# Two pixel chunks per projection to dt's input, B and C in the last layer of a four-layer kernel

## The chip, the cores and the metric

The kernel runs on one core of a Trainium2 chip. A core has a matrix engine (TensorE, PE in the profile), a vector engine (VectorE, DVE), a scalar engine (ScalarE, ACT), a general one (GpSimd, POOL) and a queue engine (SyncE, SP) that issues the DMA transfers here. The metric is device time of one execution in microseconds (us), lower is better; the number compared is the median over runs.

## The reference

Four layers follow each other on an input of 4 images with 192 channels and 56 x 56 pixels, all in fp32: an attention layer with a 7 x 7 convolution, a channel gate, a window-attention layer, and a selective scan in four directions. Only the last is touched:

```python
xn = _ln_cf(x, ln_w, ln_b)
xc, z = jnp.split(jnp.einsum('dc,bchw->bdhw', in_proj_w, xn), 2, axis=1)
xc = jax.nn.silu(depthwise_3x3(xc, conv_w) + conv_b)
x_hw = xc.reshape(Bsz, D, L)
x_wh = xc.transpose(0, 1, 3, 2).reshape(Bsz, D, L)
xs = jnp.stack([x_hw, x_wh, x_hw[..., ::-1], x_wh[..., ::-1]], axis=1)
x_dbl = jnp.einsum('kcd,bkdl->bkcl', x_proj_w, xs)
dts, Bv, Cv = jnp.split(x_dbl, [R, R + N], axis=2)
dt = jax.nn.softplus(jnp.einsum('kdr,bkrl->bkdl', dt_proj_w, dts) + dt_proj_b[None, :, :, None])
# for each pixel: h = exp(dt * A) * h + dt * B * u ; y = sum over N of h * C
ys = _selective_scan(xs, dt, A, Bv, Cv) + Ds[None, :, :, None] * xs
out = x + out_proj(layer_norm(sum over the four directions of ys) * silu(z))
```

(`depthwise_3x3`, `out_proj` and the sum over directions are written short here.) `x_dbl` is what the change is about: for each direction 12 + 4 + 4 = 20 rows, so for the two directions that run along rows (forth and back) 40 rows from the same pixels, and 40 more for the two that run along columns.

## The kernel before

All four layers are one program. Each layer's work is written as generators (threads) that yield what they need next: an engine, an estimated cost and the tiles to take. `Order` (line 270) keeps a clock of its own, at each turn picks among the first 130 threads the one that can begin earliest (a thread's place weighs 0.05 us each), and emits its instructions. The outcome is a fixed order of instructions on every engine; SP's queue gets its transfers in the order of emission. So any edit of a cost, a tile count or a condition may change the order of everything that comes after it.

In the last layer (`layer3`, line 1990) an image is cut into 7 chunks of 8 pixel rows, 448 pixels. Channels lie as two halves of 96 partitions, padded with zeros to 128.

- `begin(b, c)` (line 2103) loads one chunk of the previous layer's output, does the layer norm (L2079, L2081, L2089, L2094, L2097, L2098, L2100), the projection to x and z (L2134), the bias (L2145), the 3 x 3 convolution (L2167) and SiLU into the image's `u` (L2184), and SiLU of z (L2194), which is stored to `zmem` (L2199). The convolution's output lags by a pixel row, so the row pieces are 392, 5 x 448 and 504 pixels. Then `product` (line 2210) makes the 40 rows of `x_dbl` for that piece: two accumulating matmuls (L2218) into one PSUM bank, a copy to a `prod` tile (L2221; two such tiles, given at L2065) and a store to `prods` in DRAM (L2224). The flag `("rows", b, c)` is set.
- `begin_columns(b, c)` (line 2204) waits until all seven row pieces of the image are in, and calls `product` for eight pixel columns, read from `u` and written to the bank transposed. It sets `("columns", b, c)`.
- The scans are 28 steps per image: rows forth, columns forth, columns back, rows back, 7 chunks each. `load(t)` (line 2279) waits for the flags, for rows of chunk c also those of chunk c + 1, because of the lag; it loads dt's input (`dr`, L2289), and B and C broadcast over partitions (`bc`, L2295), from `prods`. `sizes` (line 2300) takes two steps at a time, and begins when both are loaded: matmul to dt (L2310) and softplus (L2322). `decay` (line 2337) spreads dt over the states by DMA (`da`, L2348) and takes the exponential (L2356). `scan(t, h)` (line 2359), for each half h of the channels, makes dt * u (`du`, L2371 or L2374), spreads it by matmul (L2381), multiplies by B (L2387), runs the scan on DVE (L2403), multiplies by C on POOL (L2410), sums over the states by three matmuls to three column tiles of 32 (L2426), and adds to `y` (L2431, L2436, L2440).
- `final(b, c)` (line 2227) normalises, gates by z and projects out (L2254, L2265).

The places given at lines 2452 to 2463 put `begin` of image b in the 56 half steps of image b - 1, with column products from place 48 on; for image 0 `begin` overlaps the end of the layer before.

Of the kernel before, what the change touches and what calls it, by code (L numbers as in the profile page):

```python
# [22 lines left out]
B, C, H, W = 4, 192, 56, 56  # L23
HW = H * W
HALF = 96
CH = 448
NCHUNK = HW // CH
# [214 lines left out]
def load_packs(nc, pool, packs, aps, names=None):  # L242
    tiles = {}
    for name, pack in packs.items():
        if names is not None and name not in names:
            continue
        t = pool.tile([pack.p, pack.n], F32, name=f"w_{name}", bufs=1)
        nc.sync.dma_start(t, aps[name])
        for n in pack.at:
            tiles[name + "." + n] = pack.view(t, n)  # L250
    return tiles
# [18 lines left out]
class Order:  # L270
# [29 lines left out]
    def take(self, kind="bank"):  # L300
        slot = min((s for s in self.kinds[kind] if s[0] is not None), key=lambda s: s[0])
        slot[0] = None
        return slot[1]

    def done(self, tile):

        (slot,) = (s for slots in self.kinds.values() for s in slots if s[1] is tile)
        slot[0] = self.end + self.LATENCY
# [57 lines left out]
def on_pe(n, *takes, ready=None):  # L366

    return "PE", 0.0019 * n, takes, None, ready
# [14 lines left out]
def on_act(*n, takes=(), table=None, ready=None):  # L383
    return "ACT", sum(0.2 + 0.0009 * i for i in n), takes, table, ready
# [6 lines left out]
def on_sp(*takes):  # L391
    return "SP", 0.5, takes, None, None
# [1597 lines left out]
def layer3(tc, order, pools, src, packs, aps, dst):  # L1990
# [7 lines left out]
    nc = tc.nc  # L1998
# [7 lines left out]
    w = load_packs(nc, const, packs, aps)  # L2006
# [10 lines left out]
    def keep(name, shape, n, rows=128, pool=const):  # L2017
        return [pool.tile([rows, *shape], F32, name=f"{name}{i}") for i in range(n)]

    rows = keep("row", [2, CH], 4)  # L2020
    sqs = keep("sq", [2, CH], 2)
    pads = keep("pad", [2, 11, W + 2], 2)
    us = keep("u", [2, HW], 1)
    drs = keep("dr", [SCH], 3)
# [16 lines left out]
    for m in range(4):  # L2041
        for k in range(2):
# [4 lines left out]
                start=(k == 0),  # L2047
                stop=(k == 1),
# [13 lines left out]
    yield on_dve(24, 2)  # L2062
    nc.vector.tensor_scalar_mul(a_neg, a_neg, -1.0)
    nc.vector.tensor_reduce(d_sum, w["c96.Ds"], AX.X, ALU.add)
    order.give(row=rows, sq3=sqs, dr=drs, gate=keep("gate", [2, CH], 2, HALF), prod=keep("prod", [512], 2, 40))  # L2065
    y = None
    prods = [[dram.tile([40, HW], F32, name=f"prod{b}_{o}") for o in range(2)] for b in range(B)]
    zmem = [dram.tile([C, HW], F32, name=f"zmem{b}") for b in range(B)]
    passed = set()

    def gone(*what):
        return what in passed
# [30 lines left out]
    def begin(b, c):  # L2103
# [9 lines left out]
        u = us[b % 2]  # L2113
# [4 lines left out]
        i = NCHUNK * b + c  # L2118
# [35 lines left out]
        n = y1 - y0  # L2154
        at = y0 - (8 * c - 1)
        px = slice(y0 * W, y1 * W)
        pc = None
        for t in range(9):
# [3 lines left out]
            for h in range(2):  # L2162
                for s in range(2):
                    for r in range(3):
                        o = 32 * (2 * h + s)
                        x = 28 * s + t % 3
# [4 lines left out]
                            start=(t == 0),  # L2171
                            stop=(t == 8),
                        )
        uv = u[:, :, px].rearrange("p h (y x) -> p h y x", x=W)
# [4 lines left out]
        for r in range(3):  # L2179
            yield on_act(*[28 * n] * 4, table=SILU)  # L2180
            for h in range(2):
                for s in range(2):
                    o = 32 * (2 * h + s)
# [14 lines left out]
        yield on_sp()  # L2198
        nc.sync.dma_start(pixels(zmem[b])[:, :, c * CH : (c + 1) * CH], zt)  # L2199
        done(zt)  # L2200
        yield from product(b, 0, px, u[:, :, px], 2)
        passed.add(("rows", b, c))

    def begin_columns(b, c):
        yield lambda: all(gone("rows", b, i) for i in range(NCHUNK))
        uv = us[b % 2].rearrange("p h (y x) -> p h y x", x=W)[:, :, :, 8 * c : 8 * c + 8]
        yield from product(b, 1, slice(c * CH, (c + 1) * CH), uv, 2)
        passed.add(("columns", b, c))

    def product(b, o, px, u, passes):  # L2210

        n = px.stop - px.start
        yield on_pe(passes * n, "bank")
        pp = take()

        out = pp[:40, :n].rearrange("p (x y) -> p y x", y=H) if o else pp[:40, :n]
        for k in range(2):
            nc.tensor.matmul(out, w["c128.xpT"][:, k, o], u[:, k], start=(k == 0), stop=(k == 1))  # L2218
        yield on_act(n, takes=("prod",))
        t = take("prod")  # L2220
        nc.scalar.copy(t[:, :n], pp[:40, :n])  # L2221
        done(pp)
        yield on_sp()
        nc.sync.dma_start(prods[b][o][:, px], t[:, :n])  # L2224
        done(t)

    def final(b, c):

        px = slice(c * CH, (c + 1) * CH)
        yield lambda: gone("summed", b, c) and (c == NCHUNK - 1 or gone("read", b, c + 1))  # L2230
        yield on_sp("row", "row", "gate")
        yn, xl, sz = take("row"), take("row"), take("gate")
        nc.sync.dma_start(sz, pixels(zmem[b])[:, :, px])
        yield from layer_norm(y[:, :, px], yn, read=("read", b, c))
        for h in range(2):
            yield on_act(CH)
            nc.scalar.activation(
                yn[:HALF, h],
                yn[:HALF, h],
                AF.Identity,  # L2240
                bias=w["c96.out_norm_b"][:, h : h + 1],
                scale=w["c96.out_norm_w"][:, h : h + 1],
            )
        yield on_pool(2 * CH, each=0.0021)
        nc.gpsimd.tensor_mul(yn[:HALF], yn[:HALF], sz)
        done(sz)
        yield on_sp()
        nc.sync.dma_start(xl[:HALF], pixels(src[b])[:, :, px])
        tiles = []
        for h in range(2):  # L2250
            yield on_pe(2 * CH, "bank", ready=order.end - 0.5)
            po = take()
            for k in range(2):
                nc.tensor.matmul(  # L2254
                    po[:HALF, :CH],
                    w["c128.outT"][:, k, HALF * h : HALF * h + HALF],
                    yn[:, k],
                    start=(k == 0),
                    stop=(k == 1),
                )  # L2260
            tiles.append(po)
        done(yn)
        for h in range(2):
            yield on_dve(CH)
            nc.vector.tensor_add(xl[:HALF, h], xl[:HALF, h], tiles[h][:HALF, :CH])  # L2265
            done(tiles[h])
        yield on_sp()
        nc.sync.dma_start(pixels(dst[b])[:, :, px], xl[:HALF])
        done(xl)
# [179 lines left out]
    def add(place, gen):  # L2449
        order.add(place + BASE3, gen, "3")  # L2450


    n = 8 * NSC
    for b in range(B):
        for c in range(NCHUNK):
            add(n * (b - 1) + 6 * c + 4, begin(b, c))
            add(n * (b - 1) + 48 + c, begin_columns(b, c))
            add(n * (b + 1) - 2 * c, final(b, c))
    for t in range(len(steps)):
        add(2 * t - 5, load(t))  # L2460
# [14 lines left out]
    y = late.tile([128, 2, HW], F32, name="y")  # L2475
# [13 lines left out]
def build(packs, extra):  # L2489
    nc = bacc.Bacc("TRN2", target_bir_lowering=False, num_devices=1)  # L2490

    def dram_in(name, shape):
        return nc.dram_tensor(name, shape, F32, kind="ExternalInput").ap()

    x = dram_in("x", [B, C, HW])
    aps = [{n: dram_in(n, [p.p, p.n]) for n, p in layer.items()} for layer in packs]
    aps[0].update({n: dram_in(n, list(a.shape)) for n, a in extra.items()})
    out = nc.dram_tensor("out", [B, C, HW], F32, kind="ExternalOutput").ap()
    with tile.TileContext(nc) as tc:
        with tc.tile_pool(name="between", bufs=1, space=DRAM) as dram:  # L2500
            x1 = [dram.tile([C, HW], F32, name=f"x1_{b}") for b in range(B)]
            x2 = [dram.tile([C, HW], F32, name=f"x2_{b}") for b in range(B)]
            pools = {k: ExitStack() for k in ("dram", "banks", "01", "01 sums", "2", "2 quads", "3")}
            order = layers01(tc, pools, [x[b] for b in range(B)], packs[0], aps[0], x1)
            order.add(84, layer2(tc, order, pools, x1, packs[1], aps[1], x2), "later")
            order.add(240, layer3(tc, order, pools, x2, packs[2], aps[2], [out[b] for b in range(B)]), "later")
            engines = {mybir.EngineType.PE, mybir.EngineType.Activation, mybir.EngineType.DVE, mybir.EngineType.Pool}
            with tc.manual_schedule(engines=engines):
                order.run()
            for k in ("3", "banks", "dram"):  # L2510
                pools[k].close()
    return nc
# [12 lines left out]
```

## Time and profile before

| | us |
|---|---|
| median of 3 runs | 5715.48 (5711.06 to 5721.34) |
| the profiled execution | 5731.28 |
| its span, first to last instruction | 5729.5 |
| PE busy over the span | 4866.4 (85%) |
| DVE busy over the span | 4140.6 (72%) |
| ACT busy over the span | 2655.4 (46%) |
| POOL busy over the span | 1699.9 (30%) |
| first and last matmul of L2218 begin at | 3881.4 and 5220.9 |
| first scan of the last layer (L2403) begins at | 3989.5 |

The span is the time from the first to the last instruction of one profiled execution; sums made from its rows are compared with its own time. "Busy" is the time in which an engine has at least one instruction under way. A row of the groups names a line, an engine, an operation, the tile written and the tiles read with their shapes, a count, the busy time and the mean time of one; after the bar stands the time for which the engine was idle just before, and who ended it. A chain of waits goes back from the last instruction to what released each.

### The profile page before, as it was taken

To read this page: it belongs to the slowest core of one execution; us is meant where nothing else is said; L and a number is where in the kernel's file an instruction comes from. 1 tells how busy PE (TensorE), PEld (TensorE's weight loads), DVE (VectorE), ACT (ScalarE), POOL (GpSimd) and SP (SyncE) were. 2 spreads that over 40 slices of the span, in tenths; PEclk is the share of its full clock that TensorE was granted. 3 is DMA by queue.
4 is the path that set the end of the run, shared out by engine and by line. 5 is a ranking of instruction groups with operands and counts; after the bars stand their busy time and mean duration, and the time that the engine had idled before them with its cause. 6 is when DMAs were issued, how large, how long until landed. Compare 5 with 4: busy or idle time off the path is not lost. (4 is left out here: it accounts for less than half of the span.)

```text
span 5729.5 us, 137267 instructions
## 1 busy us (share of the span) xinstructions
PE 4866.4 (85%) x58114; PEld 2407.0 (42%) x58114; DVE 4140.6 (72%) x6600; ACT 2655.4 (46%) x4271; POOL 1699.9 (30%) x1688
## 2 busy tenths in 40 slices
PE   4988998998899687898898888868888888888777
PEld 2444554454454444555555555534332232222112
DVE  5788447544744026888988888883678999998997
ACT  0122323212232215555555555546776776676544
POOL 0000000000000013433333433321345555555564
PEclk9999998999999798999999999989998999999998
DMA  6132224333332521000000000002456656566654
GB/s 185 53 80 60 66 60 105 64 88 91 76 69 56 99 77 37 14 22 21 17 22 18 19 20 21 16 26 60 122 135 157 160 145 172 155 149 167 165 149 109
DMA packets 356373, 475.97 MB, mean 83 GB/s; under 512 B 43600, under 2 KB 354256, under 8 KB 355248
## 3 DMA queue, kind: packets, MB, share of 16 engines
q1 hardware_dynamic: 355760, 467.20, 32.9%
q8 instruction: 458, 7.50, 0.5%
q14 instruction: 155, 1.27, 0.1%
HBM read 249.73 MB, written 63.17 MB: 55 GB/s over the span
## 5 line engine op out<-in xcount | busy, mean ns | idle before, releaser
L2410 POOL TENSOR_TENSOR da<-st,bc 128x448 f32<-128x448 f32 x672 | 857.0, 1281 | 751.5 <-DVE st L2403 600.1
L731 PE MATMUL bank<-X,wu 64*49 64x392 f32 x6720 | 610.5, 509 | 89.2 <-DVE X L710 85.9
L2403 DVE TENSOR_TENSOR_SCAN st<-da,st,bank 128x448 f32<-128x448 f32 x576 | 646.3, 1133 | 4.3 <-POOL da L2410 1.8
L838 POOL TENSOR_TENSOR attn<-attn,rs 112x1568 f32<-112x1568 f32 (+1 forms) x24 | 67.1, 2795 | 1726.5 <-DVE rs L836 989.9
L2356 ACT ACTIVATE da<-da,a_neg 128x448 f32<-128x448 f32 x672 | 410.1, 659 | 161.9 <-DMA da<-dt 150.2
L357 ACT ACT_TABLE_LOAD x373 | 478.6, 1283 | 6.6
L2387 DVE TENSOR_TENSOR bank<-bank,bc 128x448 f32<-128x448 f32 x672 | 382.9, 618 | 83.4 <-PE bank L2381 78.2
L731 PEld LDWEIGHTS bank<-X,wu 64*49 64x49 f32 x6720 | 247.6, 123 | 416.1 <-issue 366.4
L2426 PE MATMUL bank<-da,w_c 128*32 128x448 f32 x1344 | 348.8, 575 | 85.3 <-POOL da L2410 66.3
L2381 PE MATMUL bank<-du,w_c 32*128 32x448 f32 x1344 | 291.1, 643 | 105.2 <-DVE du L2371 59.2
L1569 DVE SCALAR_TENSOR_TENSOR bxn<-bapad,w_b,bxn 96x448 f32<-96x448 f32 (+2 forms) x448 | 318.7, 756 | 0.0
L1026 ACT ACTIVATE hm<-bank,w_a 128x448 f32<-128x448 f32 x168 | 106.3, 633 | 435.6 <-PE bank L1017 428.2
L1032 PE MATMUL bank<-hm,w_a 128*96 128x448 f32 x672 | 285.1, 555 | 16.7 <-ACT hm L1026 16.6
L1017 PE MATMUL bank<-xc,w_a 128*128 128x448 f32 x672 | 283.4, 551 | 0.6 <-DVE xc L998 0.6
L1430 POOL TENSOR_TENSOR bsq<-bsq 128x448 f32<-128x448 f32 (+7 forms) x120 | 144.5, 1206 | 446.9 <-ACT bsq L1427 401.8
L678 ACT ACTIVATE q<-bank,qk_bias,qk_scale 128x280 f32<-128x280 f32 (+2 forms) x216 | 116.9, 544 | 294.4 <-PE bank L664 251.2
L2134 PE MATMUL bank<-row,w_c 128*96 128x448 f32 x448 | 206.5, 599 | 29.7 <-DVE row L2100 27.9
L1488 PE MATMUL bank<-bxn,w_b 128*96 128x336 f32 (+2 forms) x576 | 214.3, 498 | 19.0 <-DVE bxn L1440 16.7
L754 ACT COPY sm<-bank 128x392 f32<-128x392 f32 x96 | 43.0, 489 | 380.6 <-PE bank L731 368.2
L2381 PEld LDWEIGHTS bank<-du,w_c 32*128 32x128 f32 x1344 | 92.1, 199 | 299.7 <-DVE du L2371 76.0
L998 DVE SCALAR_TENSOR_TENSOR xc<-bank,w_a,xc 96x224 f32<-96x224 f32 x112 | 44.9, 441 | 226.3 <-PE bank L988 124.5
L1763 PE MATMUL bank<-bzpad,b_diag 32*32 32x224 f32 (+2 forms) x8064 | 182.7, 371 | 24.1 <-ACT bzpad L1735 12.7
(333 smaller groups left out, 10015.4 us busy)
## 6 DMA issues: line engine op xcount, KB each, us to landing
da<-dt SPq DMA_DIRECT2D x672, 224.0 KB
vb<-vmem SPq DMA_DIRECT2D x576, 98.0 KB
bc<-prod SPq DMA_DIRECT2D x224, 224.0 KB
xq<-x SPq DMA_DIRECT2D x132, 210.0 KB
xc<-x SPq DMA_DIRECT2D x56, 336.0 KB
row<-x SPq DMA_DIRECT2D x56, 336.0 KB
xs<-x SPq DMA_DIRECT2D x28, 336.0 KB
vmem<-vt SPq DMA_DIRECT2D x56, 168.0 KB
```

The costliest lines, as they stand in the source:

```text
L357: self.nc.scalar.preload_act_table_set(table)
L731: nc.tensor.matmul(pm[a][outs[i], : WIN * W].rearrange("p (y x) -> p y x", x=W), wu[halves[a], k, dx], xt[halves[a], :, i, dx : dx + W], s ...
L1017: nc.tensor.matmul(ph[:, :CH], w["a128.c1T"][:, k, 128 * m : 128 * m + 128], xt[:, k], start=(k == 0), stop=(k == 1),)
L1032: nc.tensor.matmul(acc[h][:HALF, :CH], w["a128.c2T"][:, m, HALF * h : HALF * h + HALF], hm, start=(m == 0), stop=(m == 5),)
L1488: nc.tensor.matmul(rows2(pq[:HALF, :m]), w["b128." + wn][:, k, HALF * h : HALF * h + HALF], out[:, k], start=(k == 0), stop=(k == 1),)
L1569: nc.vector.scalar_tensor_tensor(dst, x, wt[:, t : t + 1], dst, ALU.mult, ALU.add)
L2356: nc.scalar.activation(da, da, AF.Exp, scale=a_neg[:, k, g : g + 1])
L2381: nc.tensor.matmul(tiles[j][:, :SCH], w["c96.rep"][r], du[r], start=True, stop=True)
L2387: nc.vector.tensor_mul(tiles[j][:, :SCH], tiles[j][:, :SCH], b_)
L2403: nc.vector.tensor_tensor_scan(sts[j][:, r], da[:, r], tiles[j][:, :SCH][:, r], first, ALU.mult, ALU.add)
L2410: nc.gpsimd.tensor_mul(da, sts[j], c_)
L2426: nc.tensor.matmul(py[32 * j : 32 * j + 32, :SCH], w["c128.sum"], das[j], start=True, stop=True)
```

## The change

Chunks are projected in pairs: row pieces (0, 1), (2, 3), (4, 5) and piece 6 alone, and the columns in the same way. A pair's two results lie in one bank, at partitions 0 to 39 and 64 to 103. One copy takes partitions 0 to 103 to a `prod` tile, which now has 128 partitions, and each of the two results is stored by a transfer of its own. The row piece of an even chunk is kept in `row_parts` until the next chunk's is there; flags of both are set after the pair's product. Only every second `begin_columns` is added. The order's cost for a pair on PE is that of its larger chunk.

```diff
-    order.give(row=rows, sq3=sqs, dr=drs, gate=keep("gate", [2, CH], 2, HALF), prod=keep("prod", [512], 2, 40))
+    order.give(row=rows, sq3=sqs, dr=drs, gate=keep("gate", [2, CH], 2, HALF), prod=keep("prod", [512], 2))
...
-        yield from product(b, 0, px, u[:, :, px], 2)
-        passed.add(("rows", b, c))
+        row_parts[b, c] = px, u[:, :, px]
+        both = (c - 1, c) if c % 2 else (c,)
+        if c % 2 == 0 and c < NCHUNK - 1:
+            return
+        yield from product(b, 0, [row_parts.pop((b, i)) for i in both])
+        for i in both:
+            passed.add(("rows", b, i))
+
+    row_parts = {}
...
-        uv = us[b % 2].rearrange("p h (y x) -> p h y x", x=W)[:, :, :, 8 * c : 8 * c + 8]
-        yield from product(b, 1, slice(c * CH, (c + 1) * CH), uv, 2)
-        passed.add(("columns", b, c))
+        uv = us[b % 2].rearrange("p h (y x) -> p h y x", x=W)
+        both = range(c, min(c + 2, NCHUNK))
+        yield from product(b, 1, [(slice(i * CH, (i + 1) * CH), uv[:, :, :, 8 * i : 8 * i + 8]) for i in both])
+        for i in both:
+            passed.add(("columns", b, i))
...
-    def product(b, o, px, u, passes):
-        n = px.stop - px.start
-        yield on_pe(passes * n, "bank")
+    def product(b, o, parts):
+        sizes_ = [px.stop - px.start for px, _ in parts]
+        n = max(sizes_)
+        yield on_pe(2 * n, "bank")
         pp = take()
-        out = pp[:40, :n].rearrange("p (x y) -> p y x", y=H) if o else pp[:40, :n]
         for k in range(2):
-            nc.tensor.matmul(out, w["c128.xpT"][:, k, o], u[:, k], start=(k == 0), stop=(k == 1))
+            for i, (_, u) in enumerate(parts):
+                out = pp[64 * i : 64 * i + 40, : sizes_[i]]
+                nc.tensor.matmul(
+                    out.rearrange("p (x y) -> p y x", y=H) if o else out,
+                    w["c128.xpT"][:, k, o], u[:, k], start=(k == 0), stop=(k == 1),
+                )
         yield on_act(n, takes=("prod",))
         t = take("prod")
-        nc.scalar.copy(t[:, :n], pp[:40, :n])
+        m = 64 * len(parts) - 24
+        nc.scalar.copy(t[:m, :n], pp[:m, :n])
         done(pp)
-        yield on_sp()
-        nc.sync.dma_start(prods[b][o][:, px], t[:, :n])
+        for i, (px, _) in enumerate(parts):
+            yield on_sp()
+            nc.sync.dma_start(prods[b][o][:, px], t[64 * i : 64 * i + 40, : sizes_[i]])
         done(t)
...
-            add(n * (b - 1) + 48 + c, begin_columns(b, c))
+            if c % 2 == 0:
+                add(n * (b - 1) + 48 + c, begin_columns(b, c))
```

More of the change, by code (lines that the diff above doesn't have):

```diff
@@ L2200, in begin @@
         done(zt)
-        yield from product(b, 0, px, u[:, :, px], 2)
-        passed.add(("rows", b, c))
+        row_parts[b, c] = px, u[:, :, px]
[6 more added lines that the diff above has]
+    row_parts = {}
     def begin_columns(b, c):
         yield lambda: all(gone("rows", b, i) for i in range(NCHUNK))
-        uv = us[b % 2].rearrange("p h (y x) -> p h y x", x=W)[:, :, :, 8 * c : 8 * c + 8]
-        yield from product(b, 1, slice(c * CH, (c + 1) * CH), uv, 2)
-        passed.add(("columns", b, c))
-    def product(b, o, px, u, passes):
-        n = px.stop - px.start
-        yield on_pe(passes * n, "bank")
+        uv = us[b % 2].rearrange("p h (y x) -> p h y x", x=W)
[7 more added lines that the diff above has]
+        yield on_pe(2 * n, "bank")
         pp = take()
-        out = pp[:40, :n].rearrange("p (x y) -> p y x", y=H) if o else pp[:40, :n]
         for k in range(2):
-            nc.tensor.matmul(out, w["c128.xpT"][:, k, o], u[:, k], start=(k == 0), stop=(k == 1))
+            for i, (_, u) in enumerate(parts):
+                out = pp[64 * i : 64 * i + 40, : sizes_[i]]
+                nc.tensor.matmul(
+                    out.rearrange("p (x y) -> p y x", y=H) if o else out,
+                    w["c128.xpT"][:, k, o],
+                    u[:, k],
+                    start=(k == 0),
+                    stop=(k == 1),
+                )
         yield on_act(n, takes=("prod",))
         t = take("prod")
-        nc.scalar.copy(t[:, :n], pp[:40, :n])
+        m = 64 * len(parts) - 24
+        nc.scalar.copy(t[:m, :n], pp[:m, :n])
         done(pp)
-        yield on_sp()
-        nc.sync.dma_start(prods[b][o][:, px], t[:, :n])
+        for i, (px, _) in enumerate(parts):
+            yield on_sp()
+            nc.sync.dma_start(prods[b][o][:, px], t[64 * i : 64 * i + 40, : sizes_[i]])
         done(t)
```

## The prediction

> **What bounds the kernel now.** I first read the page's busy shares, then split the last layer, where all of the change lies, into three stretches: the start-up, the stage in which later images are projected while earlier ones are scanned, and the end without projections. The columns are busy time (count), granted clock, DMA share and GB/s.
>
> ```profile
> core 0: us, PE busy (x) PEld busy (x) DVE busy (x) ACT busy (x) POOL busy (x), PEclk, DMA share, GB/s
> 3880.00:4100.00 220.00, 192.45 (x2342) 85.48 (x2340) 87.43 (x114) 137.67 (x227) 51.65 (x53) 0.94 0.32 84
> 4100.00:5250.00 1150.00, 981.35 (x7344) 325.29 (x7338) 1019.20 (x1315) 814.69 (x1262) 620.17 (x510) 0.92 0.60 153
> 5250.00:5729.50 479.50, 348.07 (x1074) 88.61 (x1074) 431.10 (x558) 232.81 (x343) 269.98 (x205) 0.90 0.55 144
> ```
>
> In the middle stage DVE (the scans) works 1019 of 1150 us and PE 981: DVE sets the pace and PE trips it. The waits of DVE there say so; the numbers are us in total, times, longest.
>
> ```profile
> DVE bank L2387 <- PE bank L2381: 53.3, 49, 3.2
> DVE y L2440 <- PE bank L2426: 26.0, 18, 5.3
> DVE row L2081 <- PE bank L2079: 21.1, 18, 4.8
> DVE y L2436 <- PE bank L2426: 8.2, 6, 1.9
> ...
> DVE row L2265 <- PE bank L2254: 6.3, 7, 2.1
> ```
>
> With 2.3 us for L2431 these make 117 of DVE's 131 idle us (1150 - 1019.2), or 89%, ended by PE. Next the chain of waits, shares by line: the middle stage has
>
> ```profile
> by line: DVE st L2403 13.4%; issue 9.3%; PE bank L2134 8.5%; PE bank L2381 8.1%; DVE bank L2387 6.4%; PE bank L2167 6.1%; PE bank L2426 5.9%; PE bank L2218 3.4%; PE bank L2254 3.4%; PE bank L2079 3.1%; PE bank L2310 3.1%; PE bank L2094 2.5%
> ```
>
> so the products (L2218) hold 3.4% of 1150 = 39.1 us of the path. Last the timeline, at the start-up's burst of column products, and the wait it leaves behind.
>
> ```profile
> 4071.09 10.72 PE L2218 MATMUL bank<-u,w_c 128*40 128x448 f32 x28
> ...
> 4087.14 0.68 DVE L2431 SCALAR_TENSOR_TENSOR y<-u,d_sum,bank 96x448 f32<-96x448 f32 x1 [12.83 <-PE bank L2426]
> ```
>
> **What goes: PE.** The groups of L2218 and of the nearest column-tiled sum, L2426, with the copy (busy us, mean ns | idle before):
>
> ```profile
> L2426 PE MATMUL bank<-da,w_c 128*32 128x448 f32 x1344 | 348.8, 575 | 85.3 <-POOL da L2410 66.3 <-DVE st L2403 15.2 <-ACT u L2184 0.9
> L2218 PE MATMUL bank<-u,w_c 128*40 128x448 f32 (+2 forms) x224 | 100.1, 579 | 1.4 <-ACT prod L2221 1.2
> L2221 ACT COPY prod<-bank 40x448 f32<-40x448 f32 (+2 forms) x56 | 29.3, 524 | 69.7 <-PE bank L2218 54.7 <-DMA prod<-prod 11.5 <-issue 1.5
> ```
>
> A product is four passes (two halves of the contraction, and the profile counts two instructions for each matmul: 224 for 112). In the starts of single instructions they follow each other by 376 ns at full clock, 407 the first time. L2426 issues three passes, to three tiles of 32 columns, within 14 ns and the next three after 386: 400 ns for three. Two tiles of 64 columns should then need between 376 and 400 ns for two passes. The 56 products become 32 (four of rows, four of columns per image), so 24 vanish: 6 in the start-up at 23.28/14 = 1.66 us, 18 in the middle stage at 76.79/42 = 1.83 us (L2218 alone, by stretch), 10.0 + 32.9 us, less 24 pairs x 4 x at most 24 ns = 2.3: some 41 us of PE. If tiles didn't overlap it would be 0.
>
> On the path of the middle stage lie 18/42 of 39.1 = 16.8 us of it. Ends: 0, if DVE's own 1019 us swallow it, and 16.8. I take 0.89 x 16.8 = **15.0**, because 89% of DVE's idle time ends with PE.
>
> **What goes: ACT.** 24 copies, x 525 ns = 12.6 us, 18 of them (9.4 us) in the stage where ACT is busy 815 of 1150 us. L754 copies 128x392 in 488 ns and L2221 40x392 to 40x504 in 468 to 572, so more partitions cost nothing. I count 0: ACT's 335 idle us hide it, and DVE's waits name ACT for under 12 us there. Without that cover it would be worth up to 9.4. The tail end of a pair's copy is not later than before: a pair takes the time of one product.
>
> [...]
>
> **What moves: the row data in the start-up.** Rows 2 and 4 of each image now wait for rows 3 and 5. For images 1 to 3 that is covered: image 1's last row product is at 4359.7, 100 us before its scans. For image 0 it is not. sizes works on steps in pairs: the first pair needs rows 2 (step 1's load), the second rows 4 (step 3's), the third rows 6. L2218 ends at 3961.43 for rows 2 and 3982.03 for rows 3; 4012.78 for rows 4 and 4034.42 for rows 5. So the scans' first pair is 20.6 us late and the second 21.6. Queued behind sizes' dt are the spreads of da on SP's queue, the exponentials on ACT and the first du on DVE (L2371 at 3980.58 before). But the third pair, from rows 6 at 4070, is where it is before, and its first du came only at 4087.74, after 12.83 us of idle DVE. Does the second pair end in time? Its load, 2.3 us after the product as before (4015.07 - 4012.78), is at 4036.7; its first du 20.2 us after that as before (4035.23 - 4015.07), at 4056.9; its four half steps take 7.1 us each at the pace just after (five from 4087.74 to 4123.10) or 8.95 at the pace just before (three from 4035.23 to 4062.09): done at 4085 to 4093. Step 4 begins 2 us earlier to 5 us later.
>
> Against that, PE loses six products there: three of the burst's seven, 4.5 us of the 10.7 for which L2426 stood behind it, and three row products, about 5. That PE time helps image 1's first projections (L2134 at 4081.74). Ends of the start-up: 4.5 + 3 = 7.5 gained (the row products by their share of the path, 61%) if the scans catch up in DVE's idle time, 21.6 lost if they don't. I take **2 gained**.
>
> **What else moves.** SP's queue still issues 56 stores, two behind one copy; prod keeps two tiles, each now with two stores to land before reuse, but half as many turns (11.5 us of ACT's wait, hidden): 0, at most 2 either way. One PSUM bank for two products instead of two: a gain at most, in a plan where banks are handed out; 0. The order on every engine is planned anew and can shift a few us either way; that goes to the range.
>
> **The clock.** Granted clock was 0.92 in the middle stage with PE busy 85% and 0.90 at the end with 73%. 33 us less PE is 2.8 points; by that slope 0.0044 of clock, 4.5 us on 949 us of PE, half of it on the path as with L2218 (39.1 of 76.8): between 0 and 4.5, I take **2 lost**.
>
> [...]
>
> **The sum.** -15.0 - 2 + 2 = -15 us. The profiled execution took 5731.28 us (span 5729.5), 15.8 us or 0.28% above the median 5715.48; I apply the difference to the median: 5700.5, **5701 us**.
>
> **Rivals.**
> (1) DVE is the bound and hides it. For it: DVE is 89% busy in the stage and 90% in the last, and PE itself waits 58 us for du (L2371, L2374) in the middle stage. Against it: the 117 us. Only the start-up's 2 us and some of the 15 remain: 5709 to 5715.
> (2) Slower: the late start isn't made up. Place: sizes of steps 0 and 1, waiting for rows 3. Price: 21.6 us, if image 0's scans stay that late; then DVE is the late engine through the stage and PE's freed time shortens no wait, at most 8 of the 15: +14 to +22, 5729 to 5737. It decides once step 4's first du comes later than about 4103, 15 us after before. For it: start-up DVE is only 40% busy because it waits on chains, and pace may not rise. Against: the 12.83 us hole.
> (3) The tiles don't overlap: pairs take eight passes in turn. PE keeps its 100 us, while the later rows cost 0 to 15: 5716 to 5730. Against: L2426.
>
> **Numbers.** Forecast 0.55, its own range 5690 (all of 16.8 and 7.5) to 5709; rivals 0.13, 0.26, 0.06. A measurement of this kernel can tell about 0.2% from no change, 11.4 us, so below 5704 is faster. Three quarters of the forecast lie there: 0.41. Its rest, rival 1 and a third of rival 3 are the same: 0.14 + 0.13 + 0.02 = 0.29. Slower 0.26 + 0.04 = 0.30. For 8 in 10 the range is 5687 to 5736: 3 below the forecast's end for a new plan, and nearly all of rival 2.
>
> **What would show it.** L2218 still x224 but busy 55 to 62 us, two starts within some 15 ns; L2221 x32 of 104 partitions, near 525 ns; the burst after 4070 6 to 7 us long; first du near 4000; step 4's first du at 4080 to 4095; DVE's idle in the projecting stage down from 131 by some 15. Wrong if L2218 stays at 100 us, if that idle time stays, or if step 4 starts after 4103.

## The result and the profile after

| | before | after |
|---|---|---|
| median of 5 runs, us | 5716.19 (5711.06 to 5725.22) | 5776.78 (5775.03 to 5784.83) |
| ratio, 95% interval | | 1.0101, 1.0090 to 1.0112 |
| the profiled execution, us | 5731.28 | 5776.78 |

The kernel became 1.0% slower, 60.6 us by the medians and 45.5 us by the two profiled executions (the one before lies 15 us above its median). Lines have moved by 10 (L2218 to L2228) to 18 (L2403 to L2421).

First the two groups that the change is about, with the columns of the page: busy us, mean ns of one, then the idle time before them.

```profile
L2228 PE MATMUL bank<-u,w_c 128*40 128x448 f32 (+2 forms) x224 | 64.2, 626 | 0.0
L2238 ACT COPY prod<-bank 104x448 f32<-104x448 f32 (+2 forms) x32 | 17.1, 533 | 48.2 <-PE bank L2228 38.1 <-DMA prod<-prod 5.8 <-ACT prod L2238 1.6
```

The products' instructions are as many as before and PE is busy with them for 64.2 us in place of 100.1; the copies are 32, and one of 104 partitions takes hardly longer than one of 40 did (533 ns against 524). What was meant to be saved was saved. Next the same three stretches of the last layer (us, then busy time and count of each engine, granted clock, DMA share, GB/s):

```profile
core 0: us, PE busy (x) PEld busy (x) DVE busy (x) ACT busy (x) POOL busy (x), PEclk, DMA share, GB/s
3880.00:4100.00 220.00, 185.91 (x2340) 83.35 (x2332) 81.47 (x107) 131.16 (x217) 47.80 (x51) 0.91 0.29 76
4100.00:5250.00 1150.00, 955.49 (x7257) 318.50 (x7256) 992.62 (x1277) 809.87 (x1232) 602.75 (x498) 0.90 0.60 149
5250.00:5775.00 525.00, 377.67 (x1181) 98.14 (x1178) 465.66 (x604) 261.59 (x381) 290.96 (x221) 0.89 0.56 143
```

In the middle stage DVE did 993 us of work in 1150, not 1019: its idle time grew from 131 to 157 us, and PE worked less too. DVE's waits there (us in total, times, longest) name the same steps as before. The first two, the spread of du and the sum over the states, have more:

```profile
DVE bank L2405 <- PE bank L2399: 65.2, 56, 2.6
DVE y L2458 <- PE bank L2444: 38.8, 18, 4.5
DVE row L2081 <- PE bank L2079: 20.6, 12, 2.4
```

These fixed stretches compare different pieces of work once one kernel is late. So I followed the starts of du, two per step of the scans, 56 per image: the k-th of one kernel is the k-th of the other. The table gives the first du, and then the time from one mark to the next (us, profiled executions).

| | first du | to half step 8 | 8 to 56 | 56 to 112 | 112 to 168 | 168 to the end |
|---|---|---|---|---|---|---|
| before | 3980.6 | 107.2 | 385.4 | 417.1 | 419.3 | 419.9 |
| after | 4005.7 | 90.6 | 377.2 | 440.5 | 436.9 | 424.1 |

Half steps 56 to 168 are the scans of images 1 and 2, beside which images 2 and 3 are projected. The late start of 25 us is made up by half step 56 (4473.5 against 4473.2), and then 23 and 18 us are lost. In that stretch the windows of before and of after are:

```profile
4473.00:5310.00 837.00, 710.33 (x5263) 235.17 (x5262) 760.69 (x982) 587.57 (x916) 462.88 (x381) 0.94 0.62 158
```

```profile
4474.00:5351.00 877.00, 730.66 (x5264) 241.45 (x5264) 761.18 (x981) 614.26 (x927) 461.44 (x380) 0.89 0.60 151
```

DVE does the same 761 us of work in 837 us and in 877. So its idle time grew from 76 to 116 us, and nearly all of that ends with PE: 64.6 us before, 102.5 after, added up over the lines that wait for PE. The two largest in these windows, before and then after:

```profile
DVE bank L2387 <- PE bank L2381: 38.3, 35, 3.2
DVE y L2440 <- PE bank L2426: 9.1, 9, 1.6
```

```profile
DVE bank L2405 <- PE bank L2399: 49.8, 42, 2.6
DVE y L2458 <- PE bank L2444: 25.7, 13, 4.5
```

All the sums together (three lines in each kernel) went from 16.8 to 37.6 us, so the late sums are more of the loss than the late spreads. PE has 20 us more of busy time, although the products gave it less to do: its granted clock fell from 0.94 to 0.89, and the time at half clock (0.5 in the records) rose from 97 to 198 us.

The timeline shows what DVE waits for. A line is start, duration, engine, instruction and count, in brackets the idle time before it and who ended it. This is a stretch of the changed kernel:

```profile
4726.22 0.96 DVE L2392 TENSOR_TENSOR du<-dt,u 96x448 f32<-96x448 f32 x1
4726.36 1.63 PE L2328 MATMUL bank<-dr,w_c 64*96 64x448 f32 x4
...
4727.92 1.78 PE L2167 MATMUL bank<-pad,diag 32*32 32x224 f32 x72
4729.64 3.25 PE L2134 MATMUL bank<-row,w_c 128*96 128x448 f32 x8
4732.81 0.95 PE L2444 MATMUL bank<-da,w_c 128*32 128x448 f32 x6
4733.69 1.00 PE L2328 MATMUL bank<-dr,w_c 64*96 64x448 f32 x4
4733.87 0.62 DVE L2458 TENSOR_TENSOR y<-y,bank 96x448 f32<-96x448 f32 x1 [4.07 <-PE bank L2444]
4734.62 1.74 PE L2079 MATMUL bank<-row,c_ones 128*96 128x448 f32 x4
4736.30 1.01 PE L2399 MATMUL bank<-du,w_c 32*128 32x448 f32 x2
...
4740.95 3.27 PE L2094 MATMUL bank<-sq,c_ones 128*96 128x448 f32 x4 [2.39 <-DVE st L2421]
```

du is ready at 4727.2, and its spread, L2399, begins at 4736.3: six other steps stand ahead of it in PE's order, 9 us of work, and DVE stands still for 4.07 us (the sum L2444 is one of the six, and comes late itself). Then PE has run ahead and idles itself (2.39 us), and a mean, whose four instructions take 1.74 us at a granted clock of 1.00 (as L2079's do here), takes 3.27 at 0.50. Before, in this stretch, the same kinds of work stand between the spreads in smaller portions:

```profile
4703.32 0.98 DVE L2374 TENSOR_TENSOR du<-dt,u 96x448 f32<-96x448 f32 x1
...
4704.44 1.03 PE L2381 MATMUL bank<-du,w_c 32*128 32x448 f32 x6 [0.48 <-DVE du L2374]
...
4705.40 2.52 PE L2167 MATMUL bank<-pad,diag 32*32 32x224 f32 x96
...
4707.85 1.29 PE L2426 MATMUL bank<-da,w_c 128*32 128x448 f32 x6
...
4709.07 1.55 PE L2167 MATMUL bank<-pad,diag 32*32 32x224 f32 x60
4709.46 1.01 DVE L2374 TENSOR_TENSOR du<-dt,u 96x448 f32<-96x448 f32 x1
...
4711.78 1.03 PE L2381 MATMUL bank<-du,w_c 32*128 32x448 f32 x6
```

So the theory: **the pairs are cheap, and the order that is planned around them is dear**. It puts the work of `begin` in lumps ahead of the two PE steps that feed DVE. The number for it is the delay from the end of a du to the start of its spread, added up over half steps 56 to 168: 166 us before, 205 after, 39 us more where the stretch takes 41 us more. It is read from one profile of each kernel.

### The profile page after: what moved, and what is told of

Its sections match the earlier page's. It is cut to its first block, busy times and chain, and to the rows that moved or that the text cites. A ratio compares the mean times of both kernels' runs of the same rounds, so it can differ in the third digit from the quotient of the medians.

```text
span 5775.0 us, 137196 instructions
## 1 busy us (share of the span) xinstructions
PE 4864.5 (84%) x58114; PEld 2405.8 (42%) x58114; DVE 4143.1 (72%) x6600; ACT 2673.6 (46%) x4267; POOL 1696.5 (29%) x1688
## 5 line engine op out<-in xcount | busy, mean ns | idle before, releaser
L2428 POOL TENSOR_TENSOR da<-st,bc 128x448 f32<-128x448 f32 x672 | 852.3, 1274 | 771.5 <-DVE st L2421 645.6
L2421 DVE TENSOR_TENSOR_SCAN st<-da,st,bank 128x448 f32<-128x448 f32 x576 | 647.3, 1134 | 5.7 <-issue 4.1
L357 ACT ACT_TABLE_LOAD x393 | 504.2, 1283 | 6.8
L2444 PE MATMUL bank<-da,w_c 128*32 128x448 f32 x1344 | 363.2, 589 | 104.7 <-POOL da L2428 76.3
L2399 PE MATMUL bank<-du,w_c 32*128 32x448 f32 x1344 | 292.5, 659 | 139.5 <-DVE du L2389 81.9
L1488 PE MATMUL bank<-bxn,w_b 128*96 128x336 f32 (+2 forms) x576 | 214.5, 499 | 19.0 <-DVE bxn L1440 16.8
L2399 PEld LDWEIGHTS bank<-du,w_c 32*128 32x128 f32 x1344 | 91.8, 202 | 332.6 <-DVE du L2389 97.4
L2444 PEld LDWEIGHTS bank<-da,w_c 128*32 128x32 f32 x1344 | 57.7, 111 | 373.6 <-POOL da L2428 258.5
```

What stands on the lines that cost most here:

```text
L357: self.nc.scalar.preload_act_table_set(table)
L2399: nc.tensor.matmul(tiles[j][:, :SCH], w["c96.rep"][r], du[r], start=True, stop=True)
L2421: nc.vector.tensor_tensor_scan(sts[j][:, r], da[:, r], tiles[j][:, :SCH][:, r], first, ALU.mult, ALU.add)
L2428: nc.gpsimd.tensor_mul(da, sts[j], c_)
L2444: nc.tensor.matmul(py[32 * j : 32 * j + 32, :SCH], w["c128.sum"], das[j], start=True, stop=True)
```

## The experiments

Each edit is against the kernel named. Ratios are to the kernel before on the same chip, with 95% intervals. "Images 1 and 2" is the time from half step 56 to 168; "delay" is the sum just defined.

### The pairs by themselves

**The order of before, with pairs.** `product` issues nothing for the first chunk of a pair and both for the second, so that the planned order of PE, DVE, ACT and POOL stays that of before (SP's queue differs in places); 18 pairs, those of images 1 to 3.

```diff
...
+        parts = [(c, px, u)]
+        if b and c < NCHUNK - 1:
+            other = kept.pop((b, o, c - 1 if c % 2 else c + 1), None)
+            if other is None:
+                kept[b, o, c] = parts[0]
+                parts = []
+            else:
+                parts.append(other)
...
         yield on_pe(passes * n, "bank")
...
```

> The pairs of images 1 to 3 are made, but the order on PE, DVE, ACT and POOL is that of before: the first chunk of a pair issues nothing, the second issues the pair (18 pairs, image 0 stays single; some 33 us less PE). Order theory (the new planned order costs the time, the pairs do not): 5700 to 5712 us, granted clock in the projecting stage near 0.94. Clock theory (less PE work lets PE fall to half clock more often): 5735 to 5780 us, with clock below 0.91 there.

**Every pair's matmuls twice**, in the order of after.

```diff
-        for k in range(2):
+        for k in (0, 1, 0, 1) if len(parts) == 2 else (0, 1):
```

> The changed kernel with the same order on PE, DVE, ACT and POOL, but each pair's four steps are computed twice into the same places, which gives PE back the 24 x 1.5 = 36 us that pairing took away. Clock theory: half-clock time in the stage of images 2 and 3 falls from 189 us towards 91, and the time to 5715 to 5745 us. Order theory: no better than the changed kernel, 5775 to 5800 us.

| | median us | ratio | images 1 and 2 | delay |
|---|---|---|---|---|
| before (its profile) | | | 836 | 166 |
| after (its profile) | 5776.78 | 1.0101 (1.0090 to 1.0112) | 877 | 205 |
| old_order | 5715.15 | 0.9988 (0.9979 to 0.9998) | 829 | 160 |
| pairs_twice | 5779.18 | 1.0099 (1.0080 to 1.0118) | 877 | 214 |

Under the old order the pairs gain 0.12% (0.02 to 0.21), some 7 us. Under the new one, doubling their matmuls (104.0 us of PE in place of 64.2) costs nothing that shows, so PE's time in the products is not what is short there. The loss is not in the pairs.

### Rows, columns, and the late start

Rows alone in pairs, columns alone in pairs (both against after), the flags of rows set late without any pair (against before), and pairs that leave image 0's rows alone (against after):

```diff
 rows_paired, in begin_columns
-        both = range(c, min(c + 2, NCHUNK))
+        both = (c,)
...
-            if c % 2 == 0:
-                add(n * (b - 1) + 48 + c, begin_columns(b, c))
+            add(n * (b - 1) + 48 + c, begin_columns(b, c))
 columns_paired, in begin
-        both = (c - 1, c) if c % 2 else (c,)
-        if c % 2 == 0 and c < NCHUNK - 1:
-            return
+        both = (c,)
 late_rows_alone, in begin
-        passed.add(("rows", b, c))
+        if c % 2 or c == NCHUNK - 1:
+            passed.add(("rows", b, c))
+            passed.add(("rows", b, c - c % 2))
 rows_late_only_after_first, in begin
-        both = (c - 1, c) if c % 2 else (c,)
-        if c % 2 == 0 and c < NCHUNK - 1:
+        both = (c - 1, c) if b and c % 2 else (c,)
+        if b and c % 2 == 0 and c < NCHUNK - 1:
             return
```

> Only the row pieces are paired (12 pairs), columns one by one; the order is planned anew. Clock theory: about half of the loss, 5735 to 5760 us. Order theory: another order, so anything from 5700 to 5790 us, with no relation to the number of pairs. Late-rows theory (row data too late somewhere): all of the loss, 5770 to 5790 us.

> Only the column pieces are paired (12 pairs), rows one by one; the order is planned anew. Clock theory: about half of the loss, 5735 to 5760 us. Order theory: anything from 5700 to 5790 us. Late-rows theory: no loss, 5700 to 5715 us.

> The kernel before, products one by one, but the row flags of a pair are set together when the second is made: the moved wait alone, with the scans' start some 20 us later. Late-rows theory (the later start drags on): the whole loss, 5760 to 5790 us. Pairing theory: 5710 to 5733 us. Chance of the order: anything from 5690 to 5775 us.

> The changed kernel with image 0's row pieces one by one, so that the scans start as early as before; rows of images 1 to 3 and all columns are paired. Late-rows theory: the loss is gone, 5695 to 5715 us. Pairing theory: the loss stays, 5760 to 5785 us. Chance of the order: anything from 5690 to 5775 us.

| | ratio | first du | half steps 8 to 56 | images 1 and 2 | delay |
|---|---|---|---|---|---|
| rows_paired | 1.0036 (1.0026 to 1.0047) | 4002.7 | 352.9 | 883 | 198 |
| columns_paired | 0.9969 (0.9959 to 0.9979) | 3981.9 | 389.3 | 824 | 154 |
| late_rows_alone | 0.9961 (0.9946 to 0.9976) | 4001.3 | 351.8 | 828 | 161 |
| rows_late_only_after_first | 1.0045 (1.0028 to 1.0062) | 3978.4 | 364.6 | 878 | 201 |

Late rows start the scans 21 us late and the kernel still becomes faster, by 0.39%: the late start isn't the cause. Without it (the last row) images 1 and 2 are as slow as in after. Of these kernels the two with pairs of rows lose, the others gain; whether the pairs themselves cost it or the plans made for them, late_even_order tells below. The effects don't add up (1.0036 and 0.9969 against 1.0101 for both), and image 0's half steps 8 to 56 take 352 to 389 us over edits that change hardly any work there: each edit gets another order.

### ScalarE's tables

The page shows another difference: the loads of function tables on ACT (L357) went from 373 to 393 in the whole program and from 102 to 126 in images 1 and 2, 1283 ns each: there softplus runs in 60 groups in place of 43. Four kernels on that: SiLU as Identity and softplus as Square, so that one table serves all of the last layer and the loads are left out, against after and against before, with the order kept; 14 extra pairs of loads within a group of softplus, against before; and softplus of a pair of steps issued together, against after.

```diff
 one_table_after, one_table_before
-                self.nc.scalar.preload_act_table_set(table)
+                want = EXP_LN if "3" in self.marks else table
+                if want != self.real:
+                    self.nc.scalar.preload_act_table_set(want)
+                self.real = want
...
-                        AF.Silu,
+                        AF.Identity if "3" in order.marks else AF.Silu,
...
-                    dts[h], tiles[h][:HALF, :SCH], AF.Softplus, bias=w["c96.dt_b"][:, h, k : k + 1]
+                    dts[h], tiles[h][:HALF, :SCH], AF.Square if "3" in order.marks else AF.Softplus, bias=w["c96.dt_b"][:, h, k : k + 1]
 extra_loads, in sizes
+                if t == ts[1] and h == 0 and b in (1, 2) and order.kept and len(splits) < 14:
+                    splits.append(t)
+                    nc.scalar.preload_act_table_set(EXP_LN)
+                    nc.scalar.preload_act_table_set(SOFTPLUS)
 batched_after, in sizes
+        held = []
...
+            held.append((t, k, tiles, b_, c_))
+        yield on_act(*[SCH] * 4, takes=("dt",) * 4, table=SOFTPLUS)
+        for t, k, tiles, b_, c_ in held:
             dts = []
             for h in range(2):
-                yield on_act(SCH, takes=("dt",), table=SOFTPLUS)
```

> The changed kernel with its order on PE, DVE, ACT and POOL, but from the moment layer 2 is over SiLU is Identity and softplus is Square, and the table loads between them are left out (173 loads instead of 394; the output is not the reference's). Table theory (the new order splits softplus into more groups, 27 more table loads in the scans of images 1 and 2, and these on ACT's queue are the loss): within 10 us of the order of before with the same cut, or faster than it. Order theory of another kind (row pieces in pairs bunch PE's work; DVE and PE wait for each other): still 30 to 60 us slower than it.

> The kernel before with the same cut: SiLU as Identity, softplus as Square and no table loads once layer 2 is over (173 instead of 374). Both theories: faster than before, by 1 to 3 us for each 2 loads left out at most, so 5450 to 5680 us; it is what the changed kernel with this cut is compared with.

> The kernel before, order kept on PE, DVE, ACT and POOL, with 28 table loads added in the scans of images 1 and 2: where four softplus stand together, two loads are put between the second and the third, 14 times. Table theory: 28 x 1.28 = 36 us more of ACT on the path, 5740 to 5765 us. Other order theory: ACT is busy 70% there and takes it, 5715 to 5730 us.

> The changed kernel, with the four softplus of two steps asked for as one piece of ACT work, so that no order can split them (planned anew). Table theory: table loads of the last layer fall from 221 to about 190, and the time to 5690 to 5720 us, no slower than before. Other order theory: no relation, 5740 to 5800 us.

| | loads | ratio | images 1 and 2 | delay |
|---|---|---|---|---|
| one_table_after | 172 | 1.0070 (1.0051 to 1.0089) | 867 | 198 |
| one_table_before | 172 | 0.9984 (0.9975 to 0.9994) | 833 | 167 |
| extra_loads | 401 | 1.0012 (1.0002 to 1.0022) | 840 | 175 |
| batched_after | 334 | 1.0032 (1.0021 to 1.0043) | 871 | 204 |

Without table loads the two orders still differ by 0.86% (1.0070 / 0.9984). 28 extra loads cost 0.12%, so 20 or 24 can't cost 1%. batched_after was planned anew too: images 1 and 2 are hardly better than in after (877), and its gain lies outside them, so it says little of the loads.

### What the plan is told

The order depends on the estimated costs. The cost of a product on PE by 0.9 and by 1.1, against before; by 0.9, against after; and a pair charged as its two products, against after:

```diff
 plan_cost_less and plan_cost_more, against before
-        yield on_pe(passes * n, "bank")
+        yield on_pe(passes * n * 0.9, "bank")
...
+        yield on_pe(passes * n * 1.1, "bank")
 pair_cost_less, against after
-        yield on_pe(2 * n, "bank")
+        yield on_pe(0.9 * 2 * n, "bank")
 charged_for_two, against after
-        yield on_pe(2 * n, "bank")
+        yield on_pe(2 * sum(sizes_), "bank")
...
-        yield on_act(n, takes=("prod",))
+        yield on_act(*sizes_, takes=("prod",))
```

> The kernel before with the same instructions; only the cost that the plan puts down for a product on PE is 0.9 of what it was, so that the order after the first products is dealt anew. Chance-of-the-order theory (each new order lands some tens of us up or down): anywhere from 5690 to 5775 us, beyond 0.2% of before. Pairing theory (row pieces in pairs are what makes a bad order): within 0.2%, 5710 to 5733 us.

> As plan_cost_less, with 1.1 of the cost. Chance-of-the-order theory: another time again, between 5690 and 5775 us, more than 0.2% from before and from plan_cost_less. Pairing theory: within 0.2% of before, 5710 to 5733 us.

> The changed kernel with 0.9 of the plan's cost for a product on PE; the order is dealt anew, with a standard deviation of 2.24 us. Uneven-order theory: 725 to 740 us for those half steps, in all 5750 to 5775 us. Chance of the order: anything from 5690 to 5790 us.

> The changed kernel, but the plan charges a pair on PE and ACT as two products, so another order is dealt; its standard deviation of PE's work per half step is 2.08 us. Uneven-order theory: half way, images 1 and 2 take some 717 us instead of 700 and 743 between the 64th and the 160th half step, in all 5705 to 5735 us. Pairing theory: 5760 to 5785 us.

And pairs of rows in all images and of columns in images 1 to 3, 21 in all, under the order of late_rows_alone (the first of a pair issues nothing, as in old_order; PE, DVE, ACT and POOL keep that kernel's order):

```diff
...
+        if (b or o == 0) and c < NCHUNK - 1:
+            other = kept.pop((b, o, c - 1 if c % 2 else c + 1), None)
...
-        passed.add(("rows", b, c))
+        if c % 2 or c == NCHUNK - 1:
+            passed.add(("rows", b, c))
+            passed.add(("rows", b, c - c % 2))
```

> Pairs (all rows, columns of images 1 to 3) in the order of late_rows_alone on PE, DVE, ACT and POOL, where PE's work between two spreads of du (L2381), counted from the order for images 1 and 2, has a standard deviation of 1.89 us against 1.86 before and 2.35 in the changed kernel. Uneven-order theory: 5680 to 5695 us, at or below late_rows_alone (5695). Pairing theory (pairs of rows cost time wherever they stand): 5740 to 5780 us.

| | median us | ratio | images 1 and 2 | delay |
|---|---|---|---|---|
| plan_cost_less | 5712.90 | 0.9991 (0.9982 to 1.0001) | 836 | 166 |
| plan_cost_more | 5715.24 | 0.9995 (0.9984 to 1.0006) | 863 | 175 |
| pair_cost_less | 5724.80 | 1.0012 (1.0003 to 1.0022) | 843 | 165 |
| charged_for_two | 5700.33 | 0.9961 (0.9946 to 0.9975) | 830 | 154 |
| late_even_order | 5692.17 | 0.9950 (0.9933 to 0.9966) | 830 | 158 |

A tenth off the product's cost, a number that no engine sees, takes 0.9% off the time of after, and charging the pair as two takes 1.4%. late_even_order has nearly all of the change's pairs and beats before and after; it doesn't differ from late_rows_alone by more than the noise. Its stretch for images 1 and 2 is

```profile
4446.00:5276.00 830.00, 697.87 (x5262) 231.06 (x5261) 760.25 (x981) 582.82 (x903) 463.00 (x381) 0.93 0.63 159
```

with PE 33 us less busy than after's 730.66, for the same work. In plan_cost_more image 2 took 440.6 us where before's took 419.3, made good by a better image 0 (357.4 us). But plan_cost_less and plan_cost_more as a whole stayed within 0.2% of before, where the theory of chance had expected more.

The expectations also used another measure, how evenly the planned order spreads PE's work over the half steps. It failed: pair_cost_less, nearly as uneven as after, was expected at 5750 to 5775 us and took 5724.80. lumped_early, below, was made slightly more even than before, was expected at 5705 to 5722 us and took 5755.90. So the evenness is not the cause.

### The clock, and lumps made by hand

**Idle PE filled**: after's order, with 36 sums over the states computed three times, in the two images' half steps where PE has least work.

```diff
+        for i in range(3 if len(sums_made) in FILL else 1):
+            for j in range(3):
+                nc.tensor.matmul(py[32 * j : 32 * j + 32, :SCH], w["c128.sum"], das[j], start=True, stop=True)
         for j in range(3):
-            nc.tensor.matmul(py[32 * j : 32 * j + 32, :SCH], w["c128.sum"], das[j], start=True, stop=True)
...
```

> The changed kernel's order; after 36 sums over the states (L2444) in images 1 and 2, where PE has under 3.2 us of work in a half step, the same sum is computed twice more into the same place, 36 x 1.6 = 58 us of PE. If the half clock after the gaps is what makes the uneven order slow: half-clock time there falls from 174 us to under 110 and the time to 5735 to 5765 us. If the lumps alone do it: no gain, 5775 to 5800 us.

**Lumps in before's order**: the convolution of images 2 and 3 is nine pieces of 24 matmuls with other work between them. All nine are issued at the place of the last (lumped_late), or of the first (lumped_early). Nothing else moves; no instruction is added.

```diff
 lumped_late
+            now = (t,) if b < 2 else range(9) if t == 8 else ()
+            for t_ in now:
...
 lumped_early
+            now = (t,) if b < 2 else range(9) if t == 0 else ()
+            for t_ in now:
...
```

> The kernel before, single products, same order of everything else; the nine pieces of a chunk's convolution (L2167) of images 2 and 3, made during the scans of images 1 and 2, all stand at the place of the ninth. PE's work per half step has a standard deviation of 2.39 us instead of 1.86, as in the changed kernel (2.35). Uneven-order theory: 725 to 745 us instead of 700 between the 64th and the 160th half step, in all 5740 to 5765 us. If unevenness only goes along with slow orders: 5710 to 5730 us.

> As lumped_late, but all nine pieces stand at the place of the first, which makes PE's work per half step slightly more even (1.74 us). Uneven-order theory: 692 to 702 us between these half steps, in all 5705 to 5722 us. If moving the convolution in one block is what costs: as lumped_late.

| | ratio | images 1 and 2 | half clock in them | delay |
|---|---|---|---|---|
| before | | 836 | 97 | 166 |
| after | 1.0101 | 877 | 198 | 205 |
| filled_gaps | 1.0123 (1.0106 to 1.0139) | 902 | 140 | 230 |
| lumped_late | 1.0116 (1.0099 to 1.0133) | 894 | 141 | 222 |
| lumped_early | 1.0068 (1.0053 to 1.0083) | 868 | 118 | 191 |

Moving one kind of PE work into lumps costs as much as the whole change, with no pair, no late row and no added load. In lumped_late's timeline a lump looks like this (the lines of both lumped kernels lie 2 after those of before):

```profile
4562.69 1.07 PE L2383 MATMUL bank<-du,w_c 32*128 32x448 f32 x6 [2.85 <-DVE du L2373]
4563.69 7.11 PE L2169 MATMUL bank<-pad,diag 32*32 32x224 f32 x216
...
4570.73 1.74 PE L2134 MATMUL bank<-row,w_c 128*96 128x448 f32 x4
4572.40 0.95 PE L2428 MATMUL bank<-da,w_c 128*32 128x448 f32 x6
...
4573.47 0.68 DVE L2433 SCALAR_TENSOR_TENSOR y<-u,d_sum,bank 96x448 f32<-96x448 f32 x1 [4.63 <-PE bank L2428]
```

The sum L2428 stands behind the 216 matmuls, and DVE idles for 4.63 us. PE itself had idled 2.85 us just before, and the lump runs slowly (the same 216 take 4.27 us elsewhere). In lumped_early it is the sums that come late. DVE's waits in images 1 and 2 at the lines of the two rows that were 9.1 and 38.3 us before:

```profile
DVE y L2442 <- PE bank L2428: 39.6, 19, 5.4
DVE bank L2389 <- PE bank L2383: 32.7, 30, 3.1
```

**The clock** is not enough by itself. filled_gaps took half-clock time from 198 to 140 us, and the kernel got no faster. That alone doesn't clear the clock, since the fillers are work too (PE's busy time there rose by 30 us). But lumped_late loses as much as after with 57 us less of half clock. And lumped_early loses 31 us in the two images with 21 more at half clock, by estimate worth at most half of that, 10 us (from the mean above, 3.27 us at 0.50 and 1.74 at 1.00). In after itself, by the same estimate, the 101 us more at half clock are worth up to 50 us of PE's time, as much as the loss there: how that loss divides between work that stands in the way and its slowness is not shown. Nor is what brings the half clock on. The granted clock is 1.0 or 0.5 in the records; of the 126 stretches at 0.5 before, 58 lasted 3.41 us and 48 lasted 6.83, and of the 133 after, 54 and 54. The 3.41 us ahead of such a stretch were seldom empty: in the last layer PE was busy in them for a median of 34% before and 38% after, at most 78%.

**All runs together.** Over the profiles of the 20 kernels the time of images 1 and 2 goes with the delay: correlation 0.97, slope 1.00, with 6 us of scatter, from 154 us of delay in 824 us (columns_paired) to 230 in 902 (filled_gaps); with the time at half clock the correlation is 0.76. Without the three kernels of this section the two correlations are 0.95 and 0.94, so over the other orders these numbers can't tell delay from clock, and the slope alone shows no cause, since a slow clock lengthens the work ahead as well. Nor is the delay the wait itself: in lumped_early the spreads stand 25 us longer and DVE waits less for them, and more for the sums. The delay marks that PE's feeding steps come late; that their place in the order costs the time is shown by the two lumped kernels, in which it was set by hand.

## Why the prediction was wrong

The forecast was 5701 and the range ended at 5736; it took 5776.78. The step that failed is this one: "The order on every engine is planned anew and can shift a few us either way; that goes to the range." The range allows for it 3 us at its lower end, and above rival 2 nothing. The runs show tens of us. With the instructions of after, but for some table loads, two other plans took 0.9961 (charged_for_two) and 1.0012 (pair_cost_less) of the time of before in place of 1.0101. Over the kernels planned anew, image 0's half steps 8 to 56 took 352 to 389 us and image 1's scans 407 to 442. In after, 41 of the 45.5 us between the two profiles were lost in images 1 and 2, 38 of them in waits of DVE that PE ended. No view that I read bounded it, and yet it got a few us: an unknown was priced as if it were small. DVE's idle time in the projecting stage, the prediction's own sign, rose from 131 to 157 us. By the other points:

- **PE's products**: 41 us less forecast, 35.9 measured (100.1 - 64.2), at a lower clock. The burst of column products was forecast at 6 to 7 us and took 6.21, in the timeline after:

```profile
4060.56 6.21 PE L2228 MATMUL bank<-u,w_c 128*40 128x448 f32 x28
```

- **-15.0 on the path** was about twice too much: under the old order 18 pairs gain some 7 us (1 to 12), and under that of late_rows_alone 21 pairs gain nothing clear of noise (0.9950 against 0.9961). Nor did it come the way that was forecast: in images 1 and 2 DVE's idle time that PE ends was 64.6 us before and 64.4 in old_order, and what ACT ends fell from 7.9 to 3.4. Rival 1, DVE hiding what PE saves, fits that. A share of the chain of waits times the saving was a bound from above and not a value.
- **ACT 0**: 17.1 us in place of 29.3, 533 ns a copy, so that a pair did not cost two copies. That their saving is worth nothing is not shown: no run tests it alone, and the waits just named hint at a few us.
- **The start-up, -2**: the first du came 25.1 us later, not 20.6. Step 4's first du came at 4096.35, 1 us past the forecast window and before 4103; by half step 56 the two kernels were level, so that 0 was gained and not 2. The catching up was right:

```profile
4096.35 0.59 DVE L2389 TENSOR_TENSOR du<-dt,u 96x448 f32<-96x448 f32 x1
```

- **Rival 2** had the sign and not the cause: its late start was made up, and alone (late_rows_alone) the kernel is 0.39% faster. **Rival 3** falls with the 64.2 us.
- **The clock, +2**: it fell by 0.05 in images 1 and 2, far more than 0.0044.

**What stays open**: why the planner, told of pairs of rows at the cost of one, deals the work in lumps. Its rule was not traced. Nor was the changed kernel's own order evened out by hand; that its order is the loss is shown by the same pairs in other orders. That it is the lumps in it rests on DVE's waits and on lumps put into before, not on undoing them in place. How late_rows_alone gains in image 0 was not followed up: it is another order, and its 352 us may be luck as after's loss is.

## What to carry to other kernels

Where a planner lays out a static order, an edit that makes one step cheaper deals the whole order anew, and that can be worth more than the step. Measure the edit under the old order first (let the removed step keep its place and its cost, and issue nothing), and charge the new step as the old ones if the plan gets worse. To judge an order, follow the same pieces of work in both traces, add up what ended the bottleneck engine's idle time there, and look at what stands ahead of the instructions that feed it.

## What the hardware showed that was not expected

- In the order in which PE waits more, the same work keeps it busy longer: in images 1 and 2 730.66 of 877 us in after and 697.87 of 830 in late_even_order, at a mean granted clock of 0.89 and 0.93. Busy time is no measure of work there; of the 35.9 us that the pairs saved, PE's total over the span shows 1.9 (4866.4 and 4864.5).
- 201 table loads of 1283 ns, 258 us of an engine that before is busy 70% of the time in images 1 and 2 (587.57 of 837), were worth 0.16% (one_table_before, where SiLU and softplus are also other functions), about 9 us: nearly all of a load is hidden here.
